# Attention of layers 1 and 3: a step's values in two halves, in a new order of score tiles, maxima and values

## The chip, the cores and the metric

The kernel runs on one core of one Trainium2 chip. The metric is the device time in microseconds of one launch, the median over several runs. Lower is better.

The engines that matter here are TensorE (PE, matmuls, with its weight loads listed apart as PEld), VectorE (DVE), ScalarE (ACT), GpSimd (POOL) and SyncE (SP, which issues most DMAs). PE reads SBUF and writes PSUM, whose eight banks hold 512 fp32 columns each for 128 partitions.

## The reference

Four layers act in turn on `x` of 1024 tokens by 128 features. Each is a cross attention with 16 heads against a context of 6404 rows, followed by a feed-forward part (mixtures of experts in layers 0, 1 and 3, a quantized one in layer 2). Only the attention of layers 1 and 3 is touched. In both, a head is 8 wide and the softmax runs over the 6404 keys:

```python
q = (query @ q_w.T + q_b).reshape(B, S, H, D).transpose(0, 2, 1, 3)
k = (key @ k_w.T + k_b).reshape(B, -1, H, D).transpose(0, 2, 1, 3)
v = (value @ v_w.T + v_b).reshape(B, -1, H, D).transpose(0, 2, 1, 3)
attn_scores = jnp.einsum('bhsd,bhtd->bhst', q, k) * SCALING
attn_weights = jax.nn.softmax(attn_scores, axis=-1)
attn_output = jnp.einsum('bhst,bhtd->bhsd', attn_weights, v)
...
x = x + _L1_xattn_ref(_layernorm(x, axis=-1), ctx_1024, ctx_1024, ...)
...
x = x + _L3_xattn_ref(_layernorm(x, axis=-1), ctx_1024, ...)
```

## The kernel before

`attn_softmax` (line 789) does the attention of one of the two layers. Its work is cut into 16 units. A unit is one pair of heads (g = 0 and 1) with one half of the queries, 512 of them. The 6404 keys are cut into 51 chunks of 128 (the last is short), and two chunks make a step, so a unit has 26 steps, and the last step has one chunk.

Three kinds of work share the steps of a unit:

- **S, a score tile.** A chunk's keys times the 512 queries of one head give a bank of scores, keys on the partitions (L1198). The contraction has 33 rows: the products in split precision and a row that subtracts the query's maximum. Head 0 sits in rows 0 to 32 of PE's array, head 1 in rows 64 to 96. Tiles alternate between a double one (`x_ps`, two banks, one buffer) and a single one (`y_ps`, one bank, one buffer), and ACT turns each into exponentials in SBUF (L1203, `px` and `py`, three buffers each). Eight tiles, four double and four single, make the twelve score banks of three steps.
- **M, a maximum.** The subtracted maxima have to be known before a unit starts, so they are made one unit ahead, from a bf16 copy: two matmuls of 64 rows, one per head, fill a tile of two banks (L970, `pair_ps`, two buffers), and DVE reduces it (L974, `mx`). A unit needs 52 of these. When the 52nd is made, `max_found` combines them, and two steps later `max_to_rows` (L1012, L1014) transposes them into the query tile `qS` of the next unit.
- **P, a step's values.** The exponentials of the step before, four banks (two chunks, two heads), are multiplied with the values (L1088). Each of the four has 32 result rows in its own quarter of the accumulator `o_ps` (one bank, one buffer), and being fp32 each is issued as two matmuls of 512 columns with their own weight loads. Eight such matmuls make one P.

Inside this stage PE, ACT and DVE run in the order in which the code is written (`tc.manual_schedule`). That order is a table of three strings, one for each step modulo three, starting anew in each unit:

```python
order = ("SMSMSP", "SMSMP", "SMSMSP")
```

After the letters of a step, one more maximum is made if the count has fallen behind two per step, and work that was put off to this step is done (`later`). When a unit's last P is done, `finish` copies `o_ps` into SBUF on ACT (L1096, `ob`), sends the sums of the exponentials through DRAM and back on SP's DMA queue, and puts off three pieces: the inverses after three steps, the scaling after six (a matmul of two rows, L1120, and a product on DVE, L1121), the projection after seven (eight matmuls, L1127, and an addition on DVE, L1131). Each of L1012, L1120 and L1127 takes a tile of the `pair_ps` ring. After eight steps the queries of the unit after next are loaded into the freed `qS`.

In a layer's last unit there are no maxima left. At each letter M the generators `beside` and, from step 9 on, `also` are advanced instead. They do the feed-forward part of the first half of the tokens (experts: L1249, L1260, L1261) and, in layer 1, prepare layer 2.

Layer 2's attention has a loop of its own. Its `values` (L1594, matmuls at L1600) already multiplies 256 columns at a time.

Of the kernel before, what the change touches and what calls it, by code (L numbers as in the profile page):

```python
# [10 lines left out]
F32 = mybir.dt.float32  # L11
# [9 lines left out]
P = 128  # L21
S = 1024
NT = S // P
HALF = 512
# [22 lines left out]
class Net:  # L47
# [741 lines left out]
    def attn_softmax(self, ctxT, L, bo, before, last, keys_early=False):  # L789
# [15 lines left out]
        NB, NK = len(blocks), len(keys)  # L805
# [5 lines left out]
        VW = 9  # L811
        KR = 33
        scale = 8.0**-0.5
        with ExitStack() as st:
# [11 lines left out]
            v = big.tile([P, NK, NH * VW + 24], F32, name="v")  # L826
# [102 lines left out]
            def load_queries(u):  # L929
                p, half = units[u]  # L930
                q = qS[u % 2]
                for g in range(2):
                    f = slice(8 * p + 64 * g, 8 * p + 64 * g + 8)
                    r = 64 * g + 32
                    nc.gpsimd.memset(q[r : r + 1].bitcast(F32), 0.0)
                    for i in range(4):
                        r = 64 * g + 8 * i
                        nc.sync.dma_start(
                            out=q[r : r + 8].bitcast(F32), in_=qd[i % 2, f, ts(half, HALF)]
                        )  # L940
# [110 lines left out]
            ps_o = self.pool(st, f"a{L}ps_o", space=PSUM)  # L1051
# [29 lines left out]
            pairs_of_keys = [[c for c in (2 * i, 2 * i + 1) if c < NK] for i in range(-(-NK // 2))]  # L1081
            STEPS = len(pairs_of_keys)

            def values(u, i, o, pts):
                for (c, g), pt in pts.items():
                    h = units[u][0] + PAIRS * g
                    j = 2 * (c % 2) + g
                    nc.tensor.matmul(  # L1088
                        o[32 * j : 32 * j + 32], v[:, c, ds(VW * h, 32)], pt,
                        start=i == 0, stop=c + 2 >= NK,  # L1090
                    )

            def out_of_banks(o):

                ob = pr.tile([P, HALF], F32, tag="ob", name="ob")
                nc.scalar.copy(ob, o)  # L1096
                dr = pr.tile([P, 2, 8], F32, tag="dr", name="dr")
                dd = dram.tile([4, HALF], F32, tag="dd", name="dd", bufs=2)
                nc.sync.dma_start(
                    out=dd, in_=ob.rearrange("(j r) n -> j r n", r=32)[:, 8]  # L1100
                )
                for par in range(2):
                    nc.sync.dma_start(
                        out=dr[:, par],
                        in_=dd[2 * par : 2 * par + 2].rearrange("g (a e) -> (g a) e", e=8),
                    )
                return ob, dr

            def inverted(dr):
                nc.vector.tensor_tensor(dr[:, 0], dr[:, 0], dr[:, 1], ALU.add)  # L1110
                nc.vector.reciprocal(dr[:, 0], dr[:, 0])
                rr = pr.tile([2, HALF], F32, tag="rr", name="rr")
                rd = dram.tile([2, HALF], F32, tag="rd", name="rd", bufs=2)
                nc.sync.dma_start(out=rd.rearrange("g (a e) -> (g a) e", e=8), in_=dr[:, 0])
                nc.sync.dma_start(out=rr, in_=rd)
                return rr

            def normalized(ob, rr):
                m = self.m_tile()
                nc.tensor.matmul(m, sel, rr, start=True, stop=True)  # L1120
                nc.vector.tensor_tensor(ob, m, ob, ALU.mult)  # L1121

            def projected(u, ob):
                p, half = units[u]
                y = self.m_tile()
                for i in range(HT):
                    nc.tensor.matmul(  # L1127
                        y[:, ts(i, P)], ob[:, ts(i, P)], wo[:, p], start=True, stop=True
                    )
                x = self.x[:, HT * half : HT * half + HT].rearrange("p t d -> p (t d)")  # L1130
                nc.vector.tensor_tensor(x, y, x, ALU.add)  # L1131

            def finish(u, o, at):

                got = {}

                def first():
                    got["ob"], got["dr"] = out_of_banks(o)

                def second():  # L1140
                    got["rr"] = inverted(got["dr"])

                def third():
                    normalized(got["ob"], got["rr"])

                def fourth():
                    projected(u, got["ob"])

                first()
                for i, f in ((3, second), (6, third), (7, fourth)):  # L1150
                    later.setdefault(at + i, []).append(f)

                def loads():
                    if u + 2 < UNITS:
                        load_queries(u + 2)
                    p, half = units[u]
                    if half and p + 2 < PAIRS:
                        load_keys(p + 2)

                later.setdefault(at + 8, []).append(loads)  # L1160

            order = ("SMSMSP", "SMSMP", "SMSMSP")
            step = 0
            waiting = []
            accs = {}
            for _ in range(ahead):
                more_max()
            also = beside = iter(())
            for u in range(UNITS):
                p = units[u][0]  # L1170
                if u == UNITS - 1:
                    pairs.close()
                    self.bank_pools(tail, f"a{L}t", h=2, m=2)
                    also, beside = last(tail, kb, kS[(PAIRS - 2) % 2])
                accs[u] = None
                pending = [(c, g) for c in range(NK) for g in range(2)]
                place = {}
                for i, cs in enumerate(pairs_of_keys):
                    for what in order[i % 3]:
                        if what == "M":  # L1180
                            more_max()
                            next(beside, None)
                            if u == UNITS - 1 and i >= 9:
                                next(also, None)
                        elif what == "S":
                            two = (len(place) % 3) == 0
                            some = [pending.pop(0) for _ in range(min(len(pending), 2 if two else 1))]
                            if not some:
                                continue
                            if two:  # L1190
                                s = ps_x.tile([P, 2, HALF], F32, tag="x", name="x_ps")
                                pt = pr.tile([P, 2, HALF], F32, tag="px", name="px", bufs=3)
                            else:
                                s = ps_y.tile([P, 1, HALF], F32, tag="y", name="y_ps")
                                pt = pr.tile([P, 1, HALF], F32, tag="py", name="py", bufs=3)
                            for k, (c, g) in enumerate(some):
                                r = slice(64 * g, 64 * g + KR)
                                nc.tensor.matmul(  # L1198
                                    s[:, k], kS[p % 2][r, ts(c, P)], qS[u % 2][r],
                                    start=True, stop=True,  # L1200
                                )
                                place[c, g] = pt[:, k]
                            nc.scalar.activation(pt[:, : len(some)], s[:, : len(some)], AF.Exp)  # L1203
                        elif waiting:
                            uu, ii, pts = waiting.pop(0)
                            if accs[uu] is None:
                                accs[uu] = ps_o.tile([P, HALF], F32, tag="o", name="o_ps")
                            values(uu, ii, accs[uu], pts)
                            if ii == STEPS - 1:
                                finish(uu, accs[uu], step)  # L1210
                    waiting.append((u, i, {(c, g): place[c, g] for c in cs for g in range(2)}))
                    if made[0] < per_unit + ahead + (step + 1) * per_unit / STEPS:
                        more_max()
                    for f in later.pop(step, ()):
                        f()
                    step += 1
            uu, ii, pts = waiting.pop(0)
            values(uu, ii, accs[uu], pts)
            finish(uu, accs[uu], step)
            for at in sorted(later):  # L1220
                for _ in range(5):
                    next(also, None)
# [860 lines left out]
```

## Time and profile before

| | |
|---|---|
| median of 3 runs | 6214.01 us (6208.23 to 6217.37) |
| the profiled execution, its own time | 6229.74 us |
| its span from first to last instruction | 6228.0 us |
| mean granted TensorE clock | 0.955 |
| loop of layer 1, by the first and last score tile | about 1191 to 2395 us |
| loop of layer 3, likewise | about 4870 to 6120 us |
| chain that ended last, costliest lines | PE o_ps L1088 5%, DVE mx L974 4%, PE x_ps L1198 3%, ACT px L1203 2% |

In a row of the page's groups stand line, engine, operation, out<-in, the shapes and the count; then the busy time in us and the mean duration of one in ns; then the idle time of the engine just before these instructions, and what ended most of it. A row of the timeline is start, duration (to the end of the last of a merged group), engine, line, operation, tiles, form and count, with the idle time before it in brackets. A row of the windows is the stretch, its length, the busy time of PE, PEld, DVE, ACT and POOL with their instruction counts, the granted TensorE clock, the DMA share and GB/s. Matmuls are pipelined: the duration of one includes its way through the array, and the distance from start to start tells what it costs the next.

### The profile page before, as it was taken

The page shows a single profiled execution, that of the slowest core. Times are in us where ns is not written, and L with a number is a line of the kernel's source. Part 1 is how long each engine was busy: PE and PEld are TensorE (multiplying, and loading weights), DVE is VectorE, ACT ScalarE, POOL GpSimd, SP SyncE. Part 2 cuts the span into 40 slices and gives each one's busy share as a digit, 9 for nine tenths or more (in the row PEclk, how much of TensorE's full clock was granted, in tenths as well). Part 3 has the DMA queues.
Part 4 walks back from the last instruction along what each step waited for, and adds up shares of the span by engine and source line. Part 5 has one row for each costly group of instructions (what it writes and reads, how often), then busy time and mean ns, then how long its engine had stood idle before and what let it go on. Part 6 is the DMA issues. An engine that isn't in the chain of part 4 may idle for free. (4 is left out here: it accounts for less than half of the span.)

```text
span 6228.0 us, 84134 instructions
## 1 busy us (share of the span) xinstructions
PE 5650.3 (91%) x33200; PEld 2170.4 (35%) x33408; DVE 4879.0 (78%) x5889; ACT 4200.3 (67%) x5228; POOL 971.8 (16%) x679
## 2 busy tenths in 40 slices
PE   6888888899999998999999988899997899999987
PEld 2333334333333334333333333333333233333335
DVE  5555553888888864799999998999997888888834
ACT  2444444477777775788888777788884677777764
POOL 4777786200000010000000000000002000000001
PEclk8999999899999998999999999999997799999978
DMA  0000002101000022000000000000002100001001
GB/s 18 2 3 2 2 1 95 31 3 25 14 13 14 13 91 89 21 15 14 13 15 14 11 12 11 11 15 13 14 11 62 35 13 13 13 13 17 11 14 41
DMA packets 139360, 130.45 MB, mean 21 GB/s; under 512 B 30750, under 2 KB 120278, under 8 KB 137983
## 3 DMA queue, kind: packets, MB, share of 16 engines
q1 hardware_dynamic: 129894, 103.35, 7.6%
q0 software_dynamic: 5296, 17.22, 0.9%
q8 instruction: 264, 4.33, 0.3%
q10 hardware_dynamic: 3760, 4.36, 0.2%
q14 instruction: 146, 1.19, 0.1%
HBM read 102.18 MB, written 35.85 MB: 22 GB/s over the span
## 5 line engine op out<-in xcount | busy, mean ns | idle before, releaser
L974 DVE TENSOR_REDUCE mx<-pair_ps 128x2 f32<-128x1024 f32 x1612 | 1811.6, 1178 | 250.4 <-PE pair_ps L970 228.4
L1203 ACT ACTIVATE px<-x_ps 128x1024 f32<-128x1024 f32 x1088 | 1113.8, 1024 | 318.7 <-PE x_ps L1198 314.4
L1592 DVE TENSOR_TENSOR e<-e,inv 128x1024 f32<-128x1024 f32 (+1 forms) x816 | 994.7, 1220 | 10.7 <-PE pair_ps L1432 0.9
L1088 PE MATMUL o_ps<-px,v 128*32 128x512 f32 x4352 | 910.8, 624 | 0.0
L1088 PE MATMUL o_ps<-py,v 128*32 128x512 f32 x2176 | 903.5, 621 | 0.0
L1441 ACT CAST lb<-pair_ps 128x1024 bf16<-128x1024 f32 (+1 forms) x714 | 720.4, 1009 | 254.3 <-PE pair_ps L1432 229.3
L970 PE MATMUL pair_ps<-kb,qz 64*128 64x512 bf16 (+1 forms) x3224 | 831.6, 388 | 54.3 <-DVE mx L974 37.4
L1203 ACT ACTIVATE py<-y_ps 128x512 f32<-128x512 f32 x1088 | 647.6, 595 | 333.0 <-PE y_ps L1198 328.6
L1535 ACT ACTIVATE e<-x_ps 128x1024 f32<-128x1024 f32 (+1 forms) x816 | 840.8, 1030 | 30.2 <-PE x_ps L1532 28.4
L1544 PE MATMUL s_ps<-e,ident 128*128 128x512 f32 (+1 forms) x1632 | 852.2, 604 | 0.4
L1198 PE MATMUL x_ps<-qS,kS 33*128 33x512 f32 x2176 | 716.3, 536 | 124.7 <-ACT px L1203 124.7
L400 POOL TENSOR_TENSOR acc<-acc,pt 128x1024 f32<-128x1024 f32 x256 | 607.0, 2371 | 68.7 <-ACT pt L389 55.5
L343 DVE TENSOR_REDUCE mx<-b_ps 128x2 f32<-128x1024 f32 (+1 forms) x306 | 342.0, 1118 | 343.5 <-PE b_ps L339 343.4
L1198 PE MATMUL y_ps<-qS,kS 33*128 33x512 f32 x1088 | 572.4, 526 | 6.2 <-ACT py L1203 6.2
L1600 PE MATMUL o_ps<-e,vz 128*32 128x256 f32 (+1 forms) x6528 | 536.5, 399 | 8.6 <-DVE e L1592 8.4
L1449 DVE TENSOR_TENSOR low<-lb,low 128x1024 bf16<-128x1024 bf16 (+1 forms) x714 | 489.4, 685 | 21.4 <-ACT lb L1441 21.2
L1532 PE MATMUL x_ps<-mneg,identb 128*128 128x512 bf16 x1424 | 454.3, 389 | 40.3 <-issue 32.9
L1528 PE MATMUL x_ps<-qS,kS 32*128 32x512 f32 x1632 | 479.1, 583 | 0.0
L389 ACT ACTIVATE pt<-x_ps,bias 128x1024 f32<-128x1024 f32 x288 | 305.2, 1110 | 235.2 <-PE x_ps L384 226.0
L1198 PEld LDWEIGHTS x_ps<-qS,kS 33*128 33x128 f32 x2176 | 286.9, 193 | 461.5 <-ACT px L1203 215.2
L970 PEld LDWEIGHTS <-qz 64*128 64x128 bf16 x3224 | 266.2, 95 | 342.4 <-issue 244.1
L1198 PEld LDWEIGHTS y_ps<-qS,kS 33*128 33x128 f32 x1088 | 208.3, 191 | 475.7 <-issue 245.4
(387 smaller groups left out, 6361.5 us busy)
## 6 DMA issues: line engine op xcount, KB each, us to landing
kS<-kst SPq DMA_DIRECT2D x400, 64.0 KB
kS<-kd SPq DMA_DIRECT2D x120, 200.1 KB
w<-in_L_ffn_w SPq DMA_DIRECT2D x48, 256.0 KB
kst<-kd POOLq DMA_DIRECT2D x24, 512.0 KB, 14.3
kd<-kh SPq DMA_DIRECT2D x12, 512.0 KB
kd<-k SPq DMA_DIRECT2D x12, 512.0 KB
qS<-qd SPq DMA_DIRECT2D x256, 16.0 KB
kb<-in_L_ffn_w SPq DMA_DIRECT2D x16, 256.0 KB
```

Source lines behind the costliest of these rows:

```text
L400: nc.gpsimd.tensor_tensor(accs[u][:n], first[:n], pt[:n], ALU.add)
L970: nc.tensor.matmul(m[:, g, :n], qzs[u][r, ts(t, P)], kb[r, at : at + n], start=True, stop=True,)
L974: nc.vector.tensor_reduce(mxs[u][:, t, b], m[:, :, :n], AX.X, ALU.max)
L1088: nc.tensor.matmul(o[32 * j : 32 * j + 32], v[:, c, ds(VW * h, 32)], pt, start=i == 0, stop=c + 2 >= NK,)
L1198: nc.tensor.matmul(s[:, k], kS[p % 2][r, ts(c, P)], qS[u % 2][r], start=True, stop=True,)
L1203: nc.scalar.activation(pt[:, : len(some)], s[:, : len(some)], AF.Exp)
L1441: nc.scalar.copy(t[:n], m[:n])
L1449: nc.vector.tensor_tensor(low[:n], t[:n], low[:n], ALU.min)
L1535: nc.scalar.activation(pair(i, k), s[:n], AF.Exp)
L1544: nc.tensor.matmul(firsts[i], self.ident[:n], es[i, h // 4][:n, h % 4], start=k == 0, stop=k == K - 1,)
L1592: nc.vector.tensor_tensor(e, e, r, ALU.mult)
L1600: nc.tensor.matmul(outs[half][32 * g : 32 * g + 32, cols], vz[i % 2][:n, ds(P * j + 32 * g, 32)], es[i, j][:n, g, cols], start=c == 0 and ...
```

## The change

A step's values are multiplied in two halves of 256 queries. The function `values` gets a `part`, 0 or 1, and works on those columns of the accumulator and of the exponentials. A new function, `half_of_values`, does one half of the oldest waiting step, and takes the step off the list, and finishes the unit, after its second half. The letter P now stands for a half, and each of the three strings has two of them. The strings hold eight S, six M and six P in three steps; the M are dealt 3, 2 and 1 where they were 2, 2 and 2.

```diff
-            def values(u, i, o, pts):
+            def values(u, i, o, pts, part):
+                cols = ts(part, HALF // 2)
                 for (c, g), pt in pts.items():
                     h = units[u][0] + PAIRS * g
                     j = 2 * (c % 2) + g
                     nc.tensor.matmul(
-                        o[32 * j : 32 * j + 32], v[:, c, ds(VW * h, 32)], pt,
-                        start=i == 0, stop=c + 2 >= NK,
+                        o[32 * j : 32 * j + 32, cols], v[:, c, ds(VW * h, 32)], pt[:, cols],
+                        start=i == 0 and part == 0, stop=c + 2 >= NK and part == 1,
                     )
...
-            order = ("SMSMSP", "SMSMP", "SMSMSP")
+            order = ("SMSPMSPM", "SMSPSMP", "SPMSP")
             step = 0
             waiting = []
             accs = {}
+
+            def half_of_values():
+                uu, ii, pts, part = waiting[0]
+                if accs[uu] is None:
+                    accs[uu] = ps_o.tile([P, HALF], F32, tag="o", name="o_ps")
+                values(uu, ii, accs[uu], pts, part)
+                if part == 0:
+                    waiting[0] = (uu, ii, pts, 1)
+                    return
+                waiting.pop(0)
+                if ii == STEPS - 1:
+                    finish(uu, accs[uu], step)
...
                         elif waiting:
-                            uu, ii, pts = waiting.pop(0)
-                            if accs[uu] is None:
-                                accs[uu] = ps_o.tile([P, HALF], F32, tag="o", name="o_ps")
-                            values(uu, ii, accs[uu], pts)
-                            if ii == STEPS - 1:
-                                finish(uu, accs[uu], step)
-                    waiting.append((u, i, {(c, g): place[c, g] for c in cs for g in range(2)}))
+                            half_of_values()
+                    waiting.append((u, i, {(c, g): place[c, g] for c in cs for g in range(2)}, 0))
...
-            uu, ii, pts = waiting.pop(0)
-            values(uu, ii, accs[uu], pts)
-            finish(uu, accs[uu], step)
+            while waiting:
+                half_of_values()
```

## The prediction

> **What bounds the kernel now.** I read the page's groups first, then the two loops of layers 1 and 3 by stretches, then one of their periods in the timeline.
>
> ```profile
> PE 5650.3 (91%) x33200; PEld 2170.4 (35%) x33408; DVE 4879.0 (78%) x5889; ACT 4200.3 (67%) x5228; POOL 971.8 (16%) x679
> ...
> L974 DVE TENSOR_REDUCE mx<-pair_ps 128x2 f32<-128x1024 f32 x1612 | 1811.6, 1178 | 250.4 <-PE pair_ps L970 228.4
> L1203 ACT ACTIVATE px<-x_ps 128x1024 f32<-128x1024 f32 x1088 | 1113.8, 1024 | 318.7 <-PE x_ps L1198 314.4
> ...
> L1198 PE MATMUL x_ps<-qS,kS 33*128 33x512 f32 x2176 | 716.3, 536 | 124.7 <-ACT px L1203 124.7
> ```
>
> No engine is full. DVE waits 228 us for the maxima's matmuls, ACT 314 us for score tiles, and PE 125 us for ACT. They wait for each other in a circle, so the order on PE decides. The timeline of layer 3 shows it; S is a score tile, M a pair of matmuls for a maximum, P a step's values.
>
> ```profile
> 5357.97 0.51 PE L1198 MATMUL x_ps<-qS,kS 33*128 33x512 f32 x2
> 5358.32 0.39 PE L970 MATMUL pair_ps<-kb,qz 64*128 64x512 bf16 x2
> 5358.36 0.58 PE L1198 MATMUL y_ps<-qS,kS 33*128 33x512 f32 x1
> 5358.58 1.02 ACT L1203 ACTIVATE px<-x_ps 128x1024 f32<-128x1024 f32 x1 [0.63 <-PE x_ps L1198]
> ...
> 5359.66 0.50 PE L1198 MATMUL x_ps<-qS,kS 33*128 33x512 f32 x2 [0.48 <-ACT px L1203]
> ...
> 5360.08 0.62 PE L1088 MATMUL o_ps<-py,v 128*32 128x512 f32 x1
> ...
> 5361.08 0.50 PE L1198 MATMUL y_ps<-qS,kS 33*128 33x512 f32 x1
> ...
> 5361.85 4.62 DVE L974 TENSOR_REDUCE mx<-pair_ps 128x2 f32<-128x1024 f32 x4 [0.74 <-PE pair_ps L970]
> ...
> 5364.26 0.39 PE L970 MATMUL pair_ps<-kb,qz 64*128 64x512 bf16 x2
> ...
> 5364.39 0.49 PE L1198 MATMUL y_ps<-qS,kS 33*128 33x512 f32 x1
> ...
> 5364.81 0.62 PE L1088 MATMUL o_ps<-px,v 128*32 128x512 f32 x1
> ...
> 5365.81 0.49 PE L1198 MATMUL x_ps<-qS,kS 33*128 33x512 f32 x2
> ```
>
> Three steps last 7.84 us here (5357.97 to 5365.81), 7.82 in most places. Their six reductions follow each other at 1.13 to 1.14 us where nothing holds them (four in 4.62 with the last one's 1.21): 6.8 us, so DVE stands for 1.0 us. It is starved while a whole P (5360.08 to 5361.08, 1.00 us) stands on PE before the next M. PE loses time at the second x tile, which waits for ACT to empty the single x bank: x to x is at least 1.69 us (0.60 to ACT's start, 1.09 from there to release).
>
> **The change part by part.** It removes 6528 value matmuls of 512 columns with their weight loads, adds 13056 of 256, and gives a step two blocks in place of one. The order becomes SMSPMSPM, SMSPSMP, SPMSP: eight S and six M per three steps as before, six half blocks for three whole ones.
>
> The price of a half block is in layer 2, whose values are already 256 columns wide, eight matmuls to a block, four columns of 32 side by side:
>
> ```profile
> 3302.68 0.64 PE L1600 MATMUL o_ps<-e,vz 128*32 128x256 f32 x8
> 3303.25 0.39 PE L1432 MATMUL pair_ps<-qn,kb 32*128 32x512 bf16 x2
> ```
>
> So 0.57 us from block to next instruction against 1.00: two halves cost 1.14, a step pays 0.14, a period 0.42. Bounds: 0.50 (exactly half) and 0.64 (the busy time of that row); I take 0.57, the same form and shape.
> The Trainium skill, "TensorE: Matmul & The Clock Gate", section Back-to-back issue gap, gives N/2.4 ns plus 2.5 ns from matmul to matmul, by which two halves stream in the time of one whole. By that rule alone the period below would be 0.4 us shorter, about 90 us over both layers; the rows show a fixed part of 0.14 us per block that the rule doesn't have.
>
> Every block also has to wait until the row-split S and M before it have left the array. Distances from the rows: fresh S to M 0.35; M to the S behind it 0.04; fresh S to block 0.42 (5359.66 to 5360.08); M, S, block 0.55 from the M (5364.26 to 5364.81); S with a second M behind it, then a block, 0.34 + 0.32; a further M and S in the same rows 0.47. With these I walk the new order from an x tile at 0:
>
> x 0, M 0.35, y 0.39, half block 0.90; M 1.47, x would start at 1.51, but x to x is 1.69: x 1.69, block 2.11; M 2.68, y, M, x would start at 3.19, ACT allows 3.38, block 3.80; y 4.37, M, block 5.03; x 5.60, block 6.02; M 6.59, y, block 7.14; next x 7.71.
>
> DVE: the six maxima arrive at 0.35, 1.47, 2.68, about 3.15, 4.37 and 6.59 and need 6.8 of 7.71: no pair tile is late by over 0.05. Exp before values: the tightest half block (0.90, on the last y tile of the step before, whose exp ends 0.1 us into the period) has 0.8 us to spare. So PE is now the bound, with 0.37 us of ACT waits left, and the period gains 7.82 - 7.71 = 0.11 us. Ends for it: with half blocks at 0.50 it is 0.53 shorter, at 0.64 it is 0.31 longer.
>
> A unit (two heads, 512 queries) has 26 steps, eight periods and two steps, and the order starts anew in each. Eight periods: -0.88. Its steps 24, 25 and 0 now carry 3 + 2 + 3 = 8 maxima, 9.0 us of DVE, where PE needs about 8.2 by the walk; two pair tiles absorb part, I take +0.5 (0 to 0.9). The last step has one chunk; its four matmuls pay two block gaps: 1.14 for 0.98, with the split order +0.2. Together -0.2 a unit. Some 28 units (14 in each layer; the others have few or no maxima) make -5 us; the gain alone would be -25.
>
> What the walk can't see is waits it leaves out; ACT has its copy of o_ps (585 ns) between exps, now with only 1.1 us between the end of a unit's last half block and the start of the next unit's first (2.68 to 3.80 of the walk): I take 0.03 us per period, +7 us (0 to 45, 0.2 per period). The copy's DMAs on SP go out a maximum earlier; the reload of queries stays eight steps behind. Maxima run ahead by one more per unit (53 for 52), up to 14: their scaling on POOL and the transposes come up to seven steps earlier, still after the reload. Nothing queues behind these for long: 0.
>
> Last unit of each layer: no maxima, expert matmuls in M's place. PE is busy 133.4 of 140 us there in layer 1 (2255 to 2395) and 141.5 of 155 in layer 3. Block gaps alone cost 26 x 0.14 = 3.6 us, double where the clock is half, and added S-to-block gaps as much: 0 to 13 us for both, taken at +6, since ACT waits hide some.
>
> Then the granted clock. Near a unit's end a two-row matmul (L1120, 1.05 us) and the projection (L1127) stand in the loop, and the clock halves:
>
> ```profile
> 5338.00:5342.00 4.00, 3.52 (x22) 1.09 (x19) 2.70 (x4) 2.54 (x3) 0.00 (x0) 1.00 0.43 55
> 5342.00:5349.00 7.00, 7.00 (x30) 3.33 (x28) 4.01 (x5) 2.25 (x4) 0.00 (x0) 0.51 0.47 59
> ```
>
> In such a stretch a block takes 1.86 us (5343.33 to 5345.19) and the projection 2.01 for 1.09; I count 11 drops in both loops, each some 3 us, 33 us in all. A drop comes when the stretch with L1120 holds little else. Half blocks stream in 0.43 of 0.57 us where whole ones do in 0.85 of 1.00, so that stretch gets thinner although waits shrink: I take two more drops, +6 us (-33 if all vanish, +51 if all 28 units have one).
> The same page's Part 1 lets the clock fall after an idle window of about 3.4 us; by that rule nothing would change here. The first row disagrees: PE was busy 3.52 of 4.00 us before this drop.
>
> Sum: -5 + 7 + 6 + 6 = +14 us. The profiled execution took 6229.74 (span 6228.0), 0.25% above the median 6214.01 of the runs; the sum is a difference of rows, so I set it on the median: 6228.
>
> **The rivals.** *Main case, 0.55: PE takes the place of DVE and ACT as the bound.* The waits fall, the blocks' gaps rise by as much: 6206 to 6262, likeliest 6228.
> *First rival, 0.30: the walk holds and the rest costs nothing.* For it: 228 us of DVE waits and 125 us of PE waits are there to be won. Each unit gains 0.88 us, or 1.36 with half blocks at 0.56 (48 of them in eight periods): 28 x 0.88 = 25, 28 x 1.36 = 38: 6176 to 6189, with the other terms at zero. It decides if a half block costs less than 0.57 and steps 24 to 0 don't stall.
> *Second rival, 0.15: the clock halves in most units.* The place is the stretch with L1120; if 24 of 28 units drop for 11 now, 13 x 3 = 39 us more: 6214 + 14 - 6 + 39 = 6261. It decides once whole units in the trace show about one drop each.
> That the order isn't carried out is excluded: PE, ACT and DVE keep program order in this stage.
>
> **How the numbers follow.** A measurement tells about 0.2%, 12 us, from no change. Main case: 0.35 above +12, 0.20 within. First rival: faster, 0.30. Second: slower, 0.15. So faster 0.30, same 0.20, slower 0.50. The range leaves out the fast half of the first rival and the slow end of the others: 6180 to 6270. Signs are mixed; the main case alone is 6206 to 6262.
>
> **What would show it.** Right: half blocks 0.57 us from their successor; a period of 7.7; L974's wait for L970 near 200 us or less and PE's wait for px well under 125; PE busy share up. A period above 7.8 in mid-unit means waits that the walk misses; one under 7.5 means that a block's fixed part is smaller here than in layer 2. Units that differ by more than a microsecond from eight periods plus 7.8 point to steps 24 to 0 or to the clock.

## The result and the profile after

The changed kernel takes 6280.53 us (median of 13 runs, 6237.95 at the lowest; the slowest, 6333.1, counts as a slow execution and is left out of the ratio) against 6215.7 us of the kernel before in the same job: a ratio of 1.0104, 95% interval 1.0079 to 1.0128. That is 65 us slower where 14 were forecast, and outside the range of 6180 to 6270. The profiled execution took 6280.53 us (span 6278.8). In the page's first part and groups, the lines that answer to those shown of before are these:

```profile
PE 5833.4 (93%) x39728; PEld 2241.5 (36%) x39936; DVE 4897.6 (78%) x5889; ACT 4230.7 (67%) x5228; POOL 971.9 (15%) x679
...
L974 DVE TENSOR_REDUCE mx<-pair_ps 128x2 f32<-128x1024 f32 x1612 | 1836.4, 1178 | 275.4 <-PE pair_ps L970 236.1
L1217 ACT ACTIVATE px<-x_ps 128x1024 f32<-128x1024 f32 x1088 | 1113.3, 1023 | 546.1 <-PE x_ps L1212 533.4
L1089 PE MATMUL o_ps<-px,v 128*32 128x256 f32 x8704 | 1111.1, 410 | 0.0
...
L1212 PE MATMUL x_ps<-qS,kS 33*128 33x512 f32 x2176 | 591.1, 527 | 6.5 <-ACT px L1217 5.2
```

The scores are at L1212 now, the exp at L1217, the values at L1089; the two-row matmul and the projection have moved by one, to L1121 and L1128. PE no longer waits for ACT (5 us, 125 before), and ACT waits for PE instead (533 us, 314 before): PE has become the bound, as the main case said. One of its signs failed: DVE's wait for the maxima was to fall to 200 us or less, and rose from 228 to 236 us. One period in the middle of a unit, from the timeline of PE (the rows of the other two value operands are left out):

```profile
5394.16 0.50 PE L1212 MATMUL x_ps<-qS,kS 33*128 33x512 f32 x2
5394.50 0.39 PE L970 MATMUL pair_ps<-kb,qz 64*128 64x512 bf16 x2
5394.54 0.58 PE L1212 MATMUL y_ps<-qS,kS 33*128 33x512 f32 x1
5395.06 0.41 PE L1089 MATMUL o_ps<-px,v 128*32 128x256 f32 x2
...
5395.62 0.39 PE L970 MATMUL pair_ps<-kb,qz 64*128 64x512 bf16 x2
5395.84 0.50 PE L1212 MATMUL x_ps<-qS,kS 33*128 33x512 f32 x2
5396.27 0.41 PE L1089 MATMUL o_ps<-px,v 128*32 128x256 f32 x2
...
5401.86 0.50 PE L1212 MATMUL x_ps<-qS,kS 33*128 33x512 f32 x2
```

Measured from the x tile at 5394.16, the M comes at 0.34, the half block at 0.90, the next M at 1.46, x at 1.68, the block at 2.11, and the period ends at 7.70. The forecast's walk had 0.35, 0.90, 1.47, 1.69, 2.11 and 7.71. From the block at 5395.06 to the M it releases are 0.56 us.

So the 65 us aren't in the pace. By the trace they are where the granted clock is half. Two places in layers 1 and 3 show it in the windows of the changed kernel (stretch, length, busy PE, PEld, DVE, ACT, POOL, then the granted clock): the first unit of layer 1, and the 15th unit of layer 3.

```profile
1235.00:1285.00 50.00, 50.00 (x276) 15.61 (x275) 26.65 (x22) 23.67 (x30) 0.00 (x0) 0.50 0.04 11
...
1307.00:1377.00 70.00, 69.32 (x633) 25.70 (x630) 62.63 (x60) 53.56 (x70) 2.60 (x3) 1.00 0.02 4
```

```profile
5932.70:5973.60 40.90, 40.22 (x366) 15.12 (x364) 32.53 (x33) 31.40 (x42) 0.00 (x0) 1.00 0.05 15
5973.60:6014.80 41.20, 41.20 (x216) 12.88 (x214) 0.69 (x1) 22.18 (x29) 0.00 (x0) 0.50 0.00 1
```

An undisturbed unit (1307 to 1377) takes 70 us at full clock. In the first unit PE runs for 50 us without a gap and gets half the clock; in the 15th it happens as soon as DVE has no more maxima (0.69 us of DVE in the second stretch). By units, from the end of one copy of `o_ps` to the next (the first from its first score tile), in the two traces: the first unit of layer 1 took 85.8 us before (24 of them at half clock) and 112.5 after (88); the 15th of layer 3 took 69.5 and 82.1 (0.5 and 41 at half clock); the last unit of layer 1 took 130.3 and 140.6, that of layer 3 153.7 and 159.1. Middle units (the second to the 14th) without a drop take 70.1 to 71.1 us after, 70.4 in the mean, against 70.4 to 71.2, 70.5 in the mean, before. Over the runs, the mean granted clock is 0.948 (median), where the kernel before has 0.958 to 0.959 in the jobs of the experiments. Without the slowest, the runs of the changed kernel lie on a line of 55 us for each 0.010 of clock; carried on to 0.958, past the highest of them at 0.955, it gives 6224 us.

### The profile page after: what moved, and what is told of

Its sections match the earlier page's. It is cut to its first block, busy times and chain, and to the rows that moved or that the text cites. A ratio compares the mean times of both kernels' runs of the same rounds, so it can differ in the third digit from the quotient of the medians.

```text
span 6278.8 us, 97185 instructions
## 1 busy us (share of the span) xinstructions
PE 5833.4 (93%) x39728; PEld 2241.5 (36%) x39936; DVE 4897.6 (78%) x5889; ACT 4230.7 (67%) x5228; POOL 971.9 (15%) x679
## 5 line engine op out<-in xcount | busy, mean ns | idle before, releaser
L974 DVE TENSOR_REDUCE mx<-pair_ps 128x2 f32<-128x1024 f32 x1612 | 1836.4, 1178 | 275.4 <-PE pair_ps L970 236.1
L1217 ACT ACTIVATE px<-x_ps 128x1024 f32<-128x1024 f32 x1088 | 1113.3, 1023 | 546.1 <-PE x_ps L1212 533.4
L1089 PE MATMUL o_ps<-px,v 128*32 128x256 f32 x8704 | 1111.1, 410 | 0.0
L1089 PE MATMUL o_ps<-py,v 128*32 128x256 f32 x4352 | 1096.1, 410 | 0.0
L970 PE MATMUL pair_ps<-kb,qz 64*128 64x512 bf16 (+1 forms) x3224 | 724.3, 391 | 35.8 <-DVE mx L974 33.0
L1217 ACT ACTIVATE py<-y_ps 128x512 f32<-128x512 f32 x1088 | 648.8, 596 | 123.6 <-PE y_ps L1212 101.1
L1212 PE MATMUL y_ps<-qS,kS 33*128 33x512 f32 x1088 | 618.9, 569 | 14.7 <-ACT py L1217 14.7
L1212 PE MATMUL x_ps<-qS,kS 33*128 33x512 f32 x2176 | 591.1, 527 | 6.5 <-ACT px L1217 5.2
L970 PEld LDWEIGHTS <-qz 64*128 64x128 bf16 x3224 | 188.0, 94 | 553.3 <-issue 529.6
L1089 PEld LDWEIGHTS o_ps<-px,v 128*32 128x32 f32 x8704 | 260.1, 110 | 326.0 <-issue 310.7
L1608 PEld LDWEIGHTS o_ps<-e,vz 128*32 128x32 f32 (+1 forms) x6528 | 132.8, 109 | 639.4 <-issue 419.3
## 6 DMA issues: line engine op xcount, KB each, us to landing
kst<-kd POOLq DMA_DIRECT2D x24, 512.0 KB, 13.7
```

The source lines that it names most:

```text
L970: nc.tensor.matmul(m[:, g, :n], qzs[u][r, ts(t, P)], kb[r, at : at + n], start=True, stop=True,)
L974: nc.vector.tensor_reduce(mxs[u][:, t, b], m[:, :, :n], AX.X, ALU.max)
L1089: nc.tensor.matmul(o[32 * j : 32 * j + 32, cols], v[:, c, ds(VW * h, 32)], pt[:, cols], start=i == 0 and part == 0, stop=c + 2 >= NK and p ...
L1212: nc.tensor.matmul(s[:, k], kS[p % 2][r, ts(c, P)], qS[u % 2][r], start=True, stop=True,)
L1608: nc.tensor.matmul(outs[half][32 * g : 32 * g + 32, cols], vz[i % 2][:n, ds(P * j + 32 * g, 32)], es[i, j][:n, g, cols], start=c == 0 and ...
```

## The experiments

Theory A: the halves cost what the forecast says and the loss is the clock, which falls where a stretch has little of the array in use, whether PE is busy or not. The rivals: B, that twice as many value matmuls cost more than the walk counts; C, that the maxima, which run ahead by one more per unit, end too early and leave PE without them in the 15th unit. A "drop" is a stretch at half clock, and a middle unit is one of the second to the 14th of a layer, 26 in both. Each ratio below is to the kernel before in the same job, and 0.001 of it is 6.2 us.

**The halves alone.** The two halves stand next to each other, in the order of before.

```diff
-            order = ("SMSPMSPM", "SMSPSMP", "SPMSP")
+            order = ("SMSMSPP", "SMSMPP", "SMSMSPP")
```

> Halves without the new order: the two half blocks of a step stand one behind the other where the whole block stood (SMSMSPP, SMSMPP, SMSMSPP). Theory A (what the change costs is time at half clock, because half blocks between other work leave PE thinner; the pace at full clock is that of before): two halves without anything between them cost no more than one whole, period 7.8 us at full clock, half-clock time in the two loops as before, 6205 to 6235 us. Rival B (each half block pays its own fixed 0.14 us wherever it stands, and the pace is what costs): period 8.2 us, about 224 x 0.42 = 94 us slower than before, 6290 to 6330.

Measured: 6216.35 us, ratio 1.0006 (0.9993 to 1.0018). The timeline of PE shows why (again with the rows of some operands left out):

```profile
5361.40 0.40 PE L1089 MATMUL o_ps<-py,v 128*32 128x256 f32 x1
...
5362.10 0.38 PE L1089 MATMUL o_ps<-py,v 128*32 128x256 f32 x1
5362.41 0.50 PE L1212 MATMUL y_ps<-qS,kS 33*128 33x512 f32 x1
```

Two adjoining halves take 1.01 us (5361.40 to 5362.41), a whole block 1.00. The fixed 0.14 us is paid only where S or M stand between the blocks. B is out.

**The order alone.** Whole blocks in the kernel before, with the new dealing of the maxima.

```diff
-            order = ("SMSMSP", "SMSMP", "SMSMSP")
+            order = ("SMSMSPM", "SMSSMP", "SMSP")
```

> The new order of score tiles and maxima with whole blocks, each where the second half stood (SMSMSPM, SMSSMP, SMSP). Theory A: the maxima dealt 3, 2, 1 do no harm to the clock, but a whole block holds PE 1.0 us in the thick of it, and by the walk the period is 7.9 to 8.1 us: 30 to 60 us slower than before, 6245 to 6275, with no long stretch at half clock in the first and the 15th unit. Rival C (the dealing of the maxima, which run out eleven steps before the end of the 15th unit, is what drops the clock): the same long half-clock stretches as in the changed kernel, and 6280 or more.

Measured: 6332.06 us, ratio 1.0192 (1.0179 to 1.0205), far above what was expected. Its page's groups:

```profile
L974 DVE TENSOR_REDUCE mx<-pair_ps 128x2 f32<-128x1024 f32 x1612 | 1822.5, 1177 | 311.7 <-PE pair_ps L970 303.2 <-PE y_ps L1198 7.4
...
L1198 PE MATMUL x_ps<-qS,kS 33*128 33x512 f32 x2176 | 627.6, 526 | 132.9 <-ACT px L1203 132.8
```

DVE waits for maxima for 303 us (236 in the changed kernel), and PE still waits 133 us for ACT. Middle units without a drop take 72.8 to 73.3 us, 2.5 more than before: 3, 2 and 1 maxima behind whole blocks starve DVE. The dealing is good only together with the halves. Both 15th units fell to half clock here too (41 and 24 us), which speaks for C as well.

**The edges as before.** The changed kernel, with units 1, 15 and 16 of each layer in whole blocks and the old order.

```diff
+            whole = ("SMSMSP", "SMSMP", "SMSMSP")
...
+                table = whole if u in (0, 14, 15) else order
```

> The changed kernel, but the first, the 15th and the last unit of each layer use the old order with whole blocks; the 13 units between keep halves and the new order. Theory A: in the traces the middle units agree at full clock (70.4 us before, 70.1 to 70.4 after) and the first unit of layer 1, the 15th of layer 3 and the last of both layers lost 55 us; with whole blocks there nearly all of it comes back: 6210 to 6235 us, mean clock 0.953 to 0.956. Rival B (the pace of half blocks in the middle units costs): 6255 to 6280.

Measured: 6248.93 us, ratio 1.0063 (1.0050 to 1.0075): 14 us above the upper end. The first and last unit came back to 89.3 and 130.4 us in layer 1, but both 15th units kept 24 and 21 us of half clock (the maxima had run out before them), and 19 of the 26 middle units had drops.

**The two-row matmul made 128 rows deep.** Zeros fill `sel` and the reciprocals, so that L1121 uses all rows of the array; what it computes is unchanged.

```diff
-            sel = big.tile([2, P], F32, name="selr")
+            sel = big.tile([P, P], F32, name="selr")
+            nc.gpsimd.memset(sel, 0.0)
+            rrs = [big.tile([P, HALF], F32, name=f"rr{i}") for i in range(2)]
+            for t in rrs:
+                nc.gpsimd.memset(t, 0.0)
...
-                rr = pr.tile([2, HALF], F32, tag="rr", name="rr")
+                rrs.append(rrs.pop(0))
+                rr = rrs[-1]
...
-                nc.sync.dma_start(out=rr, in_=rd)
+                nc.sync.dma_start(out=rr[:2], in_=rd)
```

In the changed kernel:

> The changed kernel, with the matmul at L1120 of the kernel before made 128 rows deep by zeros (the same 512 columns, the same duration). Theory A1 (the clock counts rows in use, and the two-row matmul is what drops it near each unit's end): the drops in the middle units vanish, 7 drops of 3 us and more, 20 to 35 us faster than the changed kernel; the long stretches in the first units stay. Rival A2 (the clock counts columns streamed or array time, or the zeros count for nothing): no change within 15 us, drops in the middle units as before.

In the kernel before:

> The kernel before with the L1120 matmul 128 rows deep by zeros. Theory A1 (rows in use drive the clock; the two-row matmul drops it): the 11 drops in its middle units vanish too, 11 x 2.5 to 3 us: 6175 to 6195 us, mean clock 0.961 to 0.965. Rival (the zeros helped the changed kernel for another reason, as a later start of the matmul): no change within 10 us.

Measured: 6222.31 us, ratio 1.0021 (1.0005 to 1.0037) with the change, by the ratios 52 us less than the changed kernel, more than expected; 6205.83 us, ratio 0.9988 (0.9977 to 1.0000) without it. That is a gain of 7 us where 17 to 37 were expected, and by its time alone it is what the rival expected ("no change within 10 us"); what speaks against the rival is the trace. The instruction itself costs the same. First the changed kernel's groups, then the padded one's, by line and form:

```profile
L1121 PE MATMUL pair_ps<-rr,selr 2*128 2x512 f32 x56 | 31.1, 635 | 6.4 <-DMA rr<-rd 4.2
```

```profile
L1126 PE MATMUL pair_ps<-rr,selr 128*128 128x512 f32 x56 | 31.3, 640 | 5.8 <-DMA rr<-rd 3.2 <-DVE mx L978 0.4
```

The windows show the stretch around it and what follows, in the changed kernel (L1121 at 1537.28) and in the padded one (L1126 at 1538.29):

```profile
1536.29:1539.70 3.41, 2.98 (x25) 0.96 (x17) 3.06 (x4) 1.67 (x3) 0.00 (x0) 1.00 0.61 90
1539.70:1543.11 3.41, 3.41 (x20) 1.77 (x17) 1.81 (x2) 1.28 (x2) 0.00 (x0) 0.50 0.41 65
```

```profile
1537.20:1540.61 3.41, 3.24 (x27) 1.19 (x25) 3.32 (x4) 1.79 (x3) 0.00 (x0) 1.00 0.50 60
1540.61:1554.00 13.39, 13.39 (x129) 5.43 (x125) 11.19 (x11) 9.69 (x13) 0.00 (x0) 1.00 0.26 32
```

The 13 middle units of each layer in one stretch, in the kernel before and the changed one, then in the same two with the padding:

```profile
1277.12:2204.49 927.37, 861.08 (x5516) 318.92 (x5512) 791.58 (x754) 683.18 (x898) 32.21 (x38) 0.99 0.09 14
4966.85:5897.62 930.77, 864.30 (x5516) 319.93 (x5512) 791.66 (x754) 683.02 (x898) 32.21 (x38) 0.98 0.09 14
1307.77:2242.44 934.67, 923.02 (x8194) 341.03 (x8192) 815.33 (x768) 697.26 (x899) 32.21 (x38) 0.98 0.09 14
5000.84:5932.74 931.90, 919.33 (x8194) 339.49 (x8192) 815.00 (x768) 697.09 (x899) 32.22 (x38) 0.98 0.09 14
```

```profile
1286.22:2203.47 917.25, 850.62 (x5516) 314.46 (x5512) 790.48 (x754) 682.96 (x899) 32.24 (x38) 1.00 0.10 14
4963.18:5881.70 918.52, 850.50 (x5516) 314.27 (x5512) 790.20 (x754) 682.52 (x899) 32.23 (x38) 1.00 0.10 14
1312.08:2227.13 915.05, 903.84 (x8194) 333.64 (x8192) 814.95 (x768) 696.91 (x899) 32.21 (x38) 1.00 0.10 14
4998.91:5914.47 915.56, 903.85 (x8194) 333.45 (x8192) 814.89 (x768) 696.35 (x898) 32.22 (x38) 1.00 0.09 14
```

Of these 26 units, eleven drop before, ten in the changed kernel, and none in either padded kernel. The later traces agree: none drops in any of the six with the padding, and 6 to 19 drop in each of the seven without it. So the rows in use count, and the time for which PE is busy doesn't decide. At full clock the 26 units take 1830.61 us with the change and 1835.77 without it: 0.2 us less each. What is left in the padded changed kernel is the first unit (112.5 us), both edges at the end, and 27 us at half clock in the 15th unit of layer 3.

**No further ahead.** On top of the padding, an M is left out where it would run further ahead than the kernel before lets it.

```diff
                         if what == "M":
-                            more_max()
+                            if made[0] < per_unit + ahead + 2 * step + 3:
+                                more_max()
```

> The changed kernel with the 128-row L1120, and a maximum is made at a letter M only while the count is at most three over two per step, so that maxima no longer run ahead by one per unit and last until four steps before the end of the 15th unit. Theory A: the drop of 27 to 41 us at half clock in the 15th unit (7 to 13 us of time in each layer where it came) goes, and eight maxima in three steps become seven: 10 to 25 us under the kernel with the 128-row L1120 alone, 6197 to 6213. Rival (the 15th unit drops because the half blocks are thin, not because the maxima have run out): within 6 us of 6222.

Measured: 6206.39 us, ratio 0.9994 (0.9981 to 1.0007), 16 us under the padded kernel, as expected. The windows of layer 3's 15th unit:

```profile
5871.70:5912.70 41.00, 40.89 (x376) 15.30 (x375) 36.31 (x34) 31.60 (x42) 0.00 (x0) 1.00 0.03 6
5912.70:5940.10 27.40, 26.18 (x236) 9.66 (x234) 12.36 (x14) 21.59 (x30) 0.00 (x0) 1.00 0.05 14
```

The maxima now last into the second stretch (12.36 us of DVE, 0.69 in the changed kernel), the clock stays at 1.00, and the unit takes 68.4 us. That is C: it holds too, beside A. But the guard also shortens the middle units, to 69.7 to 70.3 us:

```profile
1283.38:2191.20 907.82, 901.44 (x8166) 334.16 (x8164) 800.65 (x755) 695.56 (x898) 32.22 (x38) 1.00 0.10 14
4963.14:5871.70 908.56, 901.52 (x8166) 334.28 (x8164) 800.58 (x755) 695.28 (x898) 32.23 (x38) 1.00 0.10 14
```

The 26 of them take 1816.38 us, 14 less than in the padded kernel; the 15th unit of layer 3 takes 8.5 less (76.9 there).

**And the edges.** In addition, the first and the last unit of each layer in whole blocks and the old order; then, as a comparison, the padded kernel with only the first unit so.

```diff
+                table = whole if u in (0, 15) else order
```

> As the one before, and the first and the last unit of each layer with whole blocks in the old order. Theory A: the stay at half clock in layer 1's first unit (64 us more of it, 23 us of time) and the 10 to 15 us of the last units come back; what is left is the middle units' 70.1 to 70.4 us against 70.4: 6165 to 6190, level with or up to 10 us under the kernel before with the 128-row L1120. Rival (half blocks cost in every unit): 10 us or more over it.

> The changed kernel with the 128-row L1120 and only the first unit of each layer in the old order with whole blocks. Theory A: half blocks spread between other work keep the array so thin at half clock that the clock doesn't come back for 50 us in layer 1's first unit; without them there 15 to 27 us less than 6222: 6195 to 6207. Rival (the stay at half clock is chance or belongs to the start of the stage, whatever the blocks): within 8 us of 6222.

Measured: 6184.55 us, ratio 0.9956 (0.9939 to 0.9973) for both edges, faster than either kernel; the last unit of layer 1 takes 130.0 us again (141.9 without), that of layer 3 147.8 (141.3 without). The first unit alone: 6223.85 us, ratio 1.0013 (0.9998 to 1.0029), where 6195 to 6207 were expected: no gain that the runs can tell, although its traced first unit went from 112.5 to 89.4 us. The rival's reading holds for it.

**The guard without the padding, and two traces more.**

> The changed kernel with two-row L1120 as it is, but maxima may not run ahead by more than the kernel before lets them. Theory A (the thin stretch of L1120 and the early end of the maxima are two separate losses): only the second goes, as it did with full rows (-16 us): 6255 to 6275, the 15th units near 70 us without half clock, drops in several middle units as in the changed kernel, mean clock .949 to .951. Rival (the run-ahead itself thins the stretches in the middle units too): 6215 to 6245 and middle units nearly free of drops.

> The changed kernel once more, for a second execution's trace. If the first unit's long stay at half clock belongs to the new order: again 105 us or more with 80 us or more of half clock. If it is chance: about 89 us with 31 to 35 us. The middle units that drop, and for how long: Theory A expects five to seven per layer again, at other places, some of them with more than 10 us of half clock; the time 6240 to 6300.

> The changed kernel with L1120 on 128 rows once more, for a second execution's trace. If the first unit's long stay is chance: near 89 us here, and the time near the 6222 us median, 24 us under the first traced execution. If it belongs to the new order: 112 us again. No drop in the 28 middle units in either case; both 15th units above 75 us with 20 us or more of half clock.

Measured: 6252.68 us, ratio 1.0060 (1.0036 to 1.0084) for the guard alone, 2 us under Theory A's span and above its rival's; the 15th units take 70.5 and 68.4 us, 12 of the 26 middle units still drop. So the rows and the run-ahead are two losses: by the ratios the guard gains 27 us without the padding and 17 with it. The second trace of the changed kernel (6256.34 us) has 18 of 26 units with a drop, 27 us at half clock in layer 3's 15th unit, and a first unit of 89.1 us with 31 at half clock. The padded kernel's second trace (6254.92 us, 33 above its median) has no drop in the 26 units, both 15th units at 74.9 and 76.9 us, and a first unit of 106.5 us with 72.

The first unit is therefore partly chance: in layer 1, with halves in the new order, its half clock lasted 88, 88, 75, 72, 31 and 31 us in six traces, with whole blocks or the old order 24 to 38 us in seven; in layer 3, 32 to 76 against 32 to 35 us. What it takes to leave the state, and what that is worth in the median, stays open: the one run made for it showed no gain.

## Why the prediction missed

The ratios split the 65 us. Padding the kernel before gives -7, with an interval that reaches to no change. From there, the new order in units 2 to 15 (padded, guarded, first and last unit whole) gives 0.9956 - 0.9988, -20 us; halves in the first and last units 0.9994 - 0.9956, +23; letting the maxima run ahead 1.0021 - 0.9994, +17; the matmul with two rows 1.0104 - 1.0021, +52. Each of these four differences has an uncertainty of 13 to 18 us from its two intervals; their sum is the measured one. The shares hold for this sequence: taken away first, the run-ahead is worth 27 us, and the matmul with two rows then 41.

- **Half block and period: right.** 0.57 taken, 0.56 to 0.57 measured; 7.71 against 7.70. That a lone half pays a fixed part and adjoining halves don't is what the first experiment adds: the rule in the Trainium skill, "TensorE: Matmul & The Clock Gate", section Back-to-back issue gap, by which halving is free, agrees with the 1.01 us of two adjoining halves and not with the 0.56 us of one between other tiles.
- **Steps 24 to 0, -0.2 a unit: right.** At full clock throughout, the 26 middle units take 0.2 us less each with the change (1830.61 against 1835.77). With the guard they take another 0.55 less, about what the forecast put on these steps for eight maxima (0.5); that the guard takes away just that stall is argued.
- **Unseen waits, +7: not there.** The units show nothing left for them.
- **Maxima running ahead, priced at 0: wrong.** The step asked who queues behind them and found nobody; it didn't ask what PE does once they are all made. In layer 3's 15th unit PE is then left with scores and half blocks, and the clock halves: 8.5 us in the padded traces (76.9 against 68.4). The other 14 us that the guard gains there are the middle units' pace above; the runs have 17 for both.
- **First units: no term.** The sum counts the 28 units with maxima and the last ones. Layer 1's first unit took 26.7 us more in the first trace and 3.3 more in the second; what it is worth in the median is open.
- **Last units, +6 (0 to 13): mis-sized in layer 1.** Its last unit takes 130.0 to 130.4 us in the five traces that have the old order there, and 140.6 to 144.4 in the seven with halves in the new one, 10 to 14 more. In layer 3 the two overlap (147.8 to 153.7 and 141.3 to 159.1). First and last units together cost 23 us by the runs; how that divides between them isn't settled.
- **The clock, +6: the step that failed.** Its mechanism held: the stretch with the two-row matmul is thin, and idle time doesn't explain the drops. Its size didn't: it counted drops in one trace (11 to 13) at 3 us. The two-row matmul costs 52 us in the new order and 7 in the old, +45, give or take 20, where +6 stood; its own upper bound, +51, held it. The traces say why. Padding shortens the 26 middle units by 36 and 47 us from the changed kernel's two traces (1866.57 and 1877.77 to 1830.61), much as in the runs, but by 22 from the trace before (1858.14 to 1835.77; 2 us for each of its eleven drops), where the runs have 7. So the traced execution before, 16 us above its median, had more drops than most, and the count set on it hid most of the rise.

How many units drop depends on where they fall in time. All stretches of half clock begin and end on a grid of 3.41 us. In the trace before, L1120 starts 0.56 to 0.72 of a grid window after a grid line in the eleven units that drop, and elsewhere in the other 15. In the two traces of the changed kernel, 28 of the 38 units with a start at 0.01 to 0.56 drop, and none of the 14 at 0.63 to 0.97. So about a sixth of the window is exposed before, by which about four of 26 units would drop (an estimate, if the starts were spread evenly), and over half after.

The second rival had the mechanism and nearly the size of the clock's part (39 for 45); that its sum (6261) lies near the measured time is in part luck, since it knew nothing of the other losses. Its sign, "about one drop each", was half met. The first rival's gain, 0.88 us a unit, isn't there with the maxima as they run; with the padding and the guard it is 0.75, or 19 us in the 26 units (1816.38 against 1835.77).

## What to carry to other kernels

Splitting a block lets other work in earlier, and changes what stands beside the thinnest instruction of the loop; before counting the gain, look for that instruction, and try to fill its unused rows with zeros, which cost no time here. An effect that comes by chance, as these drops do, isn't to be counted in one trace: compare its size there with the spread of the runs. When an order produces work sooner, follow it to the end of the loop: what engine or which clock lived on it there? Whatever pays in the middle of a loop may cost in its first and last pass; choose the order for each by itself.

## What the runs showed of the hardware

The clock halves while the profile has PE busy throughout, and can stay half while PE is busy. Three drops with the window ahead of each, in the changed kernel's second trace:

```profile
5290.70:5294.10 3.40, 3.40 (x22) 1.41 (x26) 3.09 (x4) 1.94 (x4) 0.00 (x0) 1.00 0.00 0
5294.10:5297.50 3.40, 3.40 (x22) 2.13 (x18) 1.76 (x2) 0.22 (x1) 0.00 (x0) 0.50 0.00 0
5362.35:5365.75 3.40, 3.11 (x18) 1.14 (x18) 3.00 (x3) 1.68 (x4) 0.00 (x0) 1.00 0.50 68
5365.75:5369.15 3.40, 3.40 (x19) 2.27 (x18) 1.46 (x2) 0.51 (x2) 0.00 (x0) 0.50 0.55 75
5434.05:5437.45 3.40, 3.29 (x24) 1.34 (x26) 3.14 (x4) 1.94 (x4) 0.00 (x0) 1.00 0.00 0
5437.45:5440.85 3.40, 3.40 (x18) 2.20 (x18) 1.57 (x2) 0.40 (x1) 0.00 (x0) 0.50 0.00 0
```

Before the drop at 5294.10 PE was busy for all of 3.40 us. The Trainium skill, "TensorE: Matmul & The Clock Gate", Part 1, has the clock fall after an idle window of about 3.4 us and return after a busy one. The length of the window agrees: in the middle units of the changed kernel's two traces drops last 3.4, 6.8, 13.7, 17.1 or 27.3 us, that is 1, 2, 4, 5 or 8 times 3.41. The rest doesn't: the row above drops without idle time, and in the first unit 50.00 busy us out of 50.00 didn't bring the clock back. Padding the two-row matmul to 128 rows, which changes neither its duration (635 and 640 ns) nor PE's busy time by itself, removed the drops.

What counts seems to be how much of the array works in a window. As a measure I take rows times columns of the array times columns streamed, summed over the matmuls that start in it. In the trace before, the 11 windows ahead of a drop hold 0.44 to 0.69 of what the median window of the middle units holds; of the 512 others at full clock, 9 hold as little. In the changed kernel's first trace it is 0.56 to 0.71 for 10, and as little for 10 of 511.

The drops at 5294.1, 5365.75 and 5437.45 are 71.7 us apart, which is 21 times 3.41, and the units in which they stand take 71.6 to 71.9 us. So a unit that has dropped once brings the next one's thin stretch to nearly the same place in the window: L1121 starts there at 0.01, 0.09, 0.06, 0.04 and 0.06 of it in five units in a row, each with a drop. That this makes the wide scatter of the changed kernel's times is argued from these rows and wasn't tried.
